# A graph network kernel: attention of 12 node tiles by slots instead of by edges

## The chip, the cores and the metric

The kernel runs on one core of a Trainium2 chip. The core has engines that run beside one another, each with its own queue of instructions: PE multiplies matrices, DVE and ACT work on rows of 128 partitions, POOL here issues the gathers and scatters that follow a list of indices, and SP issues plain DMAs. Sixteen DMA engines move the data. The time is the device's, in microseconds (us); the kernel before took 7391.83 us, the median of three runs (7389.55 to 7428.31).

## The reference, cut to what matters

A graph has 12500 nodes with 96 features and 200000 edges, sorted by destination. Four graph layers follow one another, each with a residual and a layer norm: L0 (mean over neighbours), L1 (two rounds of sums over neighbours), L2 (attention with 8 heads of 12 features, its edges' own features included), and L3 (a softmax over neighbours per feature). The layer that changes is L2:

```
Q_h = (x @ Wq + bq).reshape(N, H, D);  K_h = ...;  V_h = ...
E = (edge_attr @ We + be).reshape(-1, H, D)
score = K_h[src] * Q_h[dst] / sqrt(D) * E
score = exp(clip(score.sum(-1, keepdims=True), -5, 5))
wV = segment_sum(V_h[src] * score, dst);  Z = segment_sum(score, dst)
h_out = wV / (Z + 1e-6)
```

## The kernel before, in words

Nodes lie in 98 tiles of 128 (`NB`), edges in 1563 tiles of 128 (`NT`). Since edges are sorted, those of node tile `d` lie in edge tiles `16d-6` to `16d+21` (`reach`). There are two ways to bring a source's row to its edge.

*By edges.* POOL gathers, for each edge tile, 128 rows from DRAM by the list of sources, one instruction per tile. A one-hot matrix, made on DVE from the destinations, is multiplied with the rows on PE and sums them into the node tile.

*By slots.* In the first stage each edge of a node tile gets a place in a table of 25 groups (`SQ`) of 128 slots. A group serves four source tiles, 32 slots each (`granule`), so that a source's row can be picked by a one-hot matrix on PE from a table in SBUF; edges that find their 32 slots full go to 64 spare slots in the last group, whose rows POOL gathers (`gather_spares`). Two one-hot matrices per node tile, `ohT` (slot to source) and `ohd` (slot to destination), are made in the first stage, stored in DRAM (`ohT_d`, `ohd_d`) and read back by later passes.

The stages follow in time:

- The first stage (`passes`, `l0_nodes`, `edge_constants`, `edge_block`, `edge_steps`, `expand`, `first_sums`). It works out L0's products, the places of all edges, the one-hots, and L0's sums: the first 76 node tiles (`NS`) by slots, the other 22 by edges (`by_edges`, "others"). `edge_steps` goes through 64 edge tiles at a time; between them, one turn of `sums` per node tile. `spare` rows are gathered per node tile, `rows_e` in runs of up to 17 tiles.
- Two L1 passes (`whole_pass`), again 76 tiles by slots, 22 by edges. In the second, `l1_stage` also makes keys and values (`kv`, stored to `kv_d` as fp32) and queries (as two fp16 halves, `q_d`) of four node tiles at a time.
- `attention`, all tiles by edges, in 391 units of four edge tiles. `ask` gathers `kv` rows on POOL 8 units ahead (L1625, 12 buffers); `fetch` reads the edges' features `attr` and queries `qs` on SP 4 units ahead; `queries` makes the one-hot `ohq` on ACT from a row of destinations. `score` multiplies on PE the edges' features with We (`ep`, L1663) and one-hots with queries (`qp`, L1667), and on DVE their product with the keys (`s`, L1671 and L1672) and its sums per head (`sc`). `weigh` takes the exponential on ACT and weighs the values on DVE (`m`, L1686), which frees the unit's `kv`. `terms` splits `m` into two fp16 halves, `one_hots_of` makes `ohe` on DVE (L1703, four instructions per unit), and `scatter` sums on PE into the node tile's accumulator (`acc`, L1719). `done` and `stage` finish four node tiles at a time: they make the layer norm, and L3's table `ex`, which goes to DRAM (`ex_d`) and into a table in SBUF (`kept[2]`).
- L3 (`whole_pass`), 68 tiles by slots (`NS3`), 30 by edges.

In attention the order of PE, DVE, ACT and POOL is written out by hand (`manual_schedule`): in turn `u`, `ask(u + 8)`, `fetch(u + 4)`, `score(u)`, `weigh(u - 1)`, `terms(u - 2)`, `one_hots_of(u - 2)`, `queries(u + 3)`, one step of a `stage`, `scatter(u - 3)`. Elsewhere a planner sets the order by its own estimates, roughly that of the program. Each engine takes its queue in order, and a wait holds up what stands behind it. Waits for data and for free buffers are put in by the framework.

Of the kernel before, what the change touches and what calls it, by code (L numbers as in the profile page):

```python
# [23 lines left out]
P = 128  # L24
N = 12500
E = 200000
D = 96
# [503 lines left out]
NS3 = 68  # L531
TS = 16 * NS + 8
# [10 lines left out]
def gnn_fast(  # L543
# [67 lines left out]
    kv_d = dram.tile([NB * P, 2 * D], F32, name="kv_d")  # L611
    q_d = dram.tile([(NB + 1) * P, 2 * D], F16, name="q_d")
# [189 lines left out]
    def l0_nodes(work, psum, pieces):  # L802
# [3 lines left out]
        for g, n in node_batches():  # L806
            xg = work.tile([P, GB, D], F32, name="x0", bufs=2)
# [11 lines left out]
            own = work.tile([P, GB, D], F32, name="own0", bufs=2)  # L819
# [32 lines left out]
    def edge_constants(big):  # L852
# [7 lines left out]
        c.first = big.tile([P, NT], BF16, name="first")  # L860
        c.cont = big.tile([P, NT], BF16, name="cont")
        c.same = big.tile([P, NT], BF16, name="same")
# [16 lines left out]
        with tc.tile_pool(name="s_ord", bufs=1) as ordp, tc.tile_pool(name="s_ordp", bufs=2, space=PSUM) as psum:  # L879
# [24 lines left out]
            last = ordp.tile([P, NT], F32, name="last")  # L904
            for j0 in range(0, NT, 512):
                n = min(512, NT - j0)
                for k, to in enumerate((c.first, last)):
                    p = psum.tile([P, 512], F32, name="p")
                    nc.tensor.matmul(p[:, :n], ones_f[0:1, :], ends[:, k, j0 : j0 + n], start=True, stop=True)
                    nc.vector.tensor_copy(to[:, j0 : j0 + n], p[:, :n])  # L910
            nc.vector.memset(c.cont[:, 0:1], 0.0)
            nc.vector.tensor_tensor(c.cont[:, 1:], c.first[:, 1:], last[:, : NT - 1], op=ALU.is_equal)
# [30 lines left out]
    def edge_block(c, blk, psum, b0):  # L943
# [27 lines left out]
        if slots:  # L971
# [4 lines left out]
            t.rearrange("t (f i) -> t f i", i=4), rowf[:, 1].rearrange("t i f -> t f i"),  # L976
# [65 lines left out]
        b.j = blk.tile([P, BL], F32, name="j")  # L1042
# [7 lines left out]
    def edge_steps(c, work, psum, t0):  # L1050
# [80 lines left out]
        pg_all = pb.rearrange("p k (g i) -> p k g i", i=UE)  # L1131

# [41 lines left out]

    def expand(work, psum, placed, d):
# [3 lines left out]
        p = psum.tile([SQ, P], F32, name="tp")  # L1179
        nc.tensor.transpose(p, lo[:, :SQ], ident)  # L1180
        r = work.tile([SQ, P], BF16, name="lorow", bufs=2)
        nc.scalar.copy(r, p)
        nc.scalar.dma_start(rowd[d], r)
# [360 lines left out]
    def l1_stage(i):  # L1544
        def stage(work, psum, g, n, sums):
# [32 lines left out]
            nc.sync.dma_start(rows(kv_d, g, n), kv[:, :n, :])  # L1578
            nc.sync.dma_start(
# [6 lines left out]
    def attention():  # L1586
# [4 lines left out]
        CQ = 16  # L1591
        with ExitStack() as c2:
            cols, within = by_columns(c2.enter_context(tc.tile_pool(name="e_cols", bufs=1)), 0, NT, F32)
# [4 lines left out]
            accp = c2.enter_context(tc.tile_pool(name="e_acc", bufs=3, space=PSUM))  # L1598
# [5 lines left out]
            for i in range(6):  # L1604
                t = one.tile([D + 1, per * P], F32, name=f"attr{i}")
                nc.vector.memset(t[D : D + 1], 1.0)
                attr.append(t)
            units = [(t0, min(per, NT - t0)) for t0 in range(0, NT, per)]
            blocks, got, asked, early, acc, held = {}, {}, {}, {}, {}, {}

            def ask_block(b):
                if b * CQ < NT:
                    n = min(CQ, NT - b * CQ)
                    qb = work.tile([P, CQ * P], BF16, name="qb")
# [3 lines left out]
            def ask(u):  # L1618

                if u >= len(units):  # L1620
                    return
                t0, n = units[u]
                kv = uw.tile([P, per, 2 * D], F32, name="kv", bufs=EARLY + 4)
                for i in range(n):
                    nc.gpsimd.indirect_dma_start(  # L1625
                        out=kv[:, i, :], out_offset=None, in_=kv_d,
                        in_offset=bass.IndirectOffsetOnAxis(ap=cols[:, t0 + i : t0 + i + 1], axis=0),
# [3 lines left out]
            def fetch(u):  # L1631
# [4 lines left out]
                if t0 % CQ == 0:  # L1636
# [7 lines left out]
            def queries(u):  # L1644
# [4 lines left out]
                b = blocks[t0 // CQ][:, t0 % CQ * P : (t0 % CQ + n) * P]  # L1649
# [5 lines left out]

            def score(u):
                t0, n = units[u]
                a, qs = got.pop(u)
                ohq = asked.pop(u)
                kv = early.pop(u)  # L1660
                ep = psum.tile([P, per, D], F32, name="ep")
                for i in range(n):
                    nc.tensor.matmul(ep[:, i, :], a[:, i * P : (i + 1) * P], w_e, start=True, stop=True)  # L1663
                qp = psum.tile([P, per, D], F32, name="qp")
                for i in range(n):
# [4 lines left out]
                s = uw.tile([P, per, D], F32, name="s")  # L1670
                nc.vector.tensor_mul(s[:, :n, :], ep[:, :n, :], kv[:, :n, :D])  # L1671
                nc.vector.tensor_mul(s[:, :n, :], s[:, :n, :], qp[:, :n, :])  # L1672
                sc = uw.tile([P, per, HEADS], F32, name="sc", bufs=3)
                nc.vector.tensor_reduce(sc[:, :n, :], s[:, :n, :].rearrange("p e (h d) -> p e h d", d=HD), AX.X, ALU.add)  # L1674
                nc.vector.scalar_tensor_tensor(  # L1675
                    sc[:, :n, :], sc[:, :n, :], -5.0, five[:, :n, :], op0=ALU.max, op1=ALU.min
                )
                return n, kv, sc

            def weigh(n, kv, sc):  # L1680
# [3 lines left out]
                m = uw.tile([P, per, HEADS, H1], F32, name="m")  # L1684
                nc.scalar.mul(m[:, :n, :, HD], ex[:, :n, :], 2.0**8)
                nc.vector.tensor_mul(  # L1686
                    m[:, :n, :, :HD], kv[:, :n, D:].rearrange("p e (h d) -> p e h d", d=HD),
                    ex[:, :n, :, None].to_broadcast([P, n, HEADS, HD]),
                )
                return n, m.rearrange("p e h d -> p e (h d)")  # L1690

            def terms(n, m):
# [4 lines left out]
                return mh  # L1697

            def one_hots_of(u):
                t0, n = units[u]  # L1700
                o = uw.tile([P, per, 2 * P], BF16, name="ohe")
                for i in range(n):
                    nc.vector.tensor_scalar(o[:, i], wide, within[:, t0 + i : t0 + i + 1], None, op0=ALU.is_equal)  # L1703
                return o

            def scatter(u, m, ohe):
                t0, n = units[u]
                for i in range(n):
                    t = t0 + i
                    for k in range(2):  # L1710
                        d = nominal(t) + k
                        if not 0 <= d < NB:
# [13 lines left out]
            def done(d, a):  # L1726
# [258 lines left out]
```

## Time and profile before

The profiled execution took 7449.54 us; its span, from the first to the last instruction, is 7447.7 us. Times of the stages come from the windows view, whose columns give each engine's busy time.

| stage, us from the span's start | length | PE | DVE | ACT | POOL | clock granted to PE |
|---|---|---|---|---|---|---|
| first stage, 230 to 1575 | 1345 | 912.90 | 935.12 | 683.47 | 559.16 | 0.75 |
| L1, first pass, 1575 to 2560 | 985 | 634.62 | 372.07 | 283.31 | 399.24 | 0.75 |
| L1, second pass, 2560 to 3520 | 960 | 644.77 | 432.20 | 312.76 | 352.65 | 0.76 |
| attention, 3520 to 6075 | 2555 | 1376.31 | 1621.20 | 1007.41 | 1531.94 | 0.58 |
| L3, 6075 to 7448 | 1373 | 1004.79 | 636.33 | 454.79 | 496.37 | 0.80 |

A row of the windows view reads: start and end, length, then for each engine its busy time and its instructions (x), the granted share of PE's clock, the busy share of the DMA engines and their GB/s. A row of the view of waits reads: who waited, `<-`, for whom; total us, times, longest. A row of the timeline reads: start, duration, engine, line, operation, what it writes `<-` what it reads, how many, and in brackets how long the engine had been idle and who ended that. "Issue" means that the engine waited for nothing that the profile shows, "remote" that the releaser is unknown.

### The profile page before, as it was taken

What the parts mean: (1) busy time and instruction counts of PE and PEld (TensorE: products, weight loads), DVE (VectorE), ACT (ScalarE), POOL (GpSimd) and SP (SyncE); (2) the same over time, 40 slices, a digit from 0 to 9 for tenths busy, and PEclk for the clock granted to TensorE, in tenths of its full rate; (3) what the DMA queues carried; (4) which work ended last, traced back from release to release, by engine and by line L of the source; (5) the groups of instructions that cost most, each with busy time, mean ns of one, the idle gap of its engine ahead of it and who ended that gap; (6) DMA issues with size and microseconds to landing.
All of it is one profiled execution on the core that took longest, in us unless ns stands there. A gap on an engine that the chain in (4) does not pass through costs nothing.

```text
span 7447.7 us, 155952 instructions
## 1 busy us (share of the span) xinstructions
PE 4699.1 (63%) x63527; PEld 3396.2 (46%) x63527; DVE 4164.5 (56%) x9977; ACT 2805.0 (38%) x5549; POOL 3345.9 (45%) x3338
## 2 busy tenths in 40 slices
PE   5566776746666566666355555555555547777777
PEld 3454554534545444445344444444444434444444
DVE  7577777623434344445466666666666654444545
ACT  2454555523323233333244443444343433333333
POOL 0434444434343344332666565666666643333332
PEclk8677777767777777777555565655555658878888
DMA  4555555443434344444344444444444433333332
GB/s 104 151 163 167 163 167 165 149 116 103 112 99 112 96 110 112 118 119 130 109 129 130 125 131 127 130 132 127 128 130 130 131 90 90 88 88 90 90 89 62
DMA packets 656952, 894.05 MB, mean 120 GB/s; under 512 B 394162, under 2 KB 458885, under 8 KB 651357
## 3 DMA queue, kind: packets, MB, share of 16 engines
q1 hardware_dynamic: 498742, 615.02, 27.2%
q0 software_dynamic: 138784, 262.63, 14.3%
q8 instruction: 500, 8.19, 0.5%
q10 hardware_dynamic: 18695, 6.32, 0.4%
q14 instruction: 231, 1.89, 0.1%
HBM read 747.72 MB, written 135.87 MB: 119 GB/s over the span
## 4 chain that ended last, share of the span: by engine, by line
PE 29%; DVE 22%; another core or an unknown queue 15%; issue 13%; ACT 2%; POOL 1%; DMA 1%; DVEq 0%; ACTq 0%; SPq 0%; POOLq 0%
PE rows L1438 9%; PE acc L1449 7%; DVE ohe L1703 3%; PE acc L1369 3%; DVE s L1672 3%; DVE sc L1674 3%; DVE mh L1696 2%; DVE s L1671 2%; DVE msg L1441 2%; PE ep L1663 2%; PE acc L1719 2%; PE qp L1667 1%; POOL kv L1625 1%; DVE m L1686 1%
## 5 line engine op out<-in xcount | busy, mean ns | idle before, releaser
L1625 POOL DMA_INDIRECT kv<-kv_d,cols x1563 | 1531.4, 980 | 964.3 <-DVE m L1686 464.6
L1438 PE MATMUL rows<-tab,ohT 128*32 128x192 f16 (+1 forms) x21560 | 1114.2, 294 | 696.0 <-issue 610.9
L1441 ACT CAST msg<-rows 128x384 f16<-128x384 f32 (+1 forms) x1440 | 877.2, 641 | 1775.4 <-remote 1041.7
L1441 DVE CAST msg<-rows 128x768 f16<-128x768 f32 x720 | 686.7, 954 | 1478.7 <-remote 1008.1
L1383 POOL DMA_INDIRECT rows_e<-tab_d,cols x1065 | 1105.0, 1038 | 658.9 <-PE acc L1369 349.2
L1438 PEld LDWEIGHTS <-ohT 128*32 128x32 fp8e4 x21560 | 596.2, 101 | 1123.1 <-issue 1044.0
L1449 PE MATMUL acc<-msg,ohd 128*32 128x384 f16 (+1 forms) x10600 | 928.3, 324 | 247.8 <-issue 241.0
L1719 PE MATMUL acc<-mh,ohe 128*128 128x208 f16 x2727 | 516.3, 352 | 844.2 <-DVE ohe L1703 517.8
L1449 PEld LDWEIGHTS <-ohd 128*32 128x32 fp8e4 (+1 forms) x10600 | 554.0, 103 | 526.9 <-issue 434.7
L1719 PEld LDWEIGHTS <-ohe 128*128 128x128 bf16 x2727 | 293.3, 124 | 1011.0 <-DVE ohe L1703 575.5
L1663 PE MATMUL ep<-w_e,attr 97*128 97x96 f32 x3126 | 664.5, 382 | 35.3 <-issue 31.7
L1663 PEld LDWEIGHTS ep<-w_e,attr 97*128 97x128 f32 x3126 | 631.4, 297 | 37.6 <-issue 26.3
L1383 POOL DMA_INDIRECT rows_e<-ex_d,cols x483 | 464.2, 961 | 399.0 <-PE acc L1369 261.9
L1683 ACT ACTIVATE ex<-sc 128x32 f32<-128x32 f32 x391 | 89.7, 229 | 1440.5 <-DVE sc L1675 1166.9
L1303 ACT CAST msg<-rows 128x768 f16<-128x768 f32 x633 | 384.2, 644 | 459.8 <-PE rows L1299 224.6
L1671 DVE TENSOR_TENSOR s<-ep,kv 128x384 f32<-128x384 f32 x391 | 215.6, 551 | 604.7 <-remote 307.1
L1313 PE MATMUL acc<-msg,ohd 128*32 128x194 f16 x7600 | 389.3, 291 | 252.4 <-ACT msg L1303 177.9
L1667 PE MATMUL qp<-qs,ohq 128*128 128x96 f16 x3126 | 352.5, 260 | 292.9 <-issue 270.0
L1667 PEld LDWEIGHTS <-ohq 128*128 128x128 fp8e4 x3126 | 295.4, 136 | 339.4 <-issue 336.4
L1299 PE MATMUL rows<-tab,ohT 128*32 128x192 f16 x7448 | 393.9, 289 | 61.5 <-issue 59.6
L1242 POOL DMA_INDIRECT spare<-tab_d,spare_i x76 | 132.3, 1740 | 656.3 <-PE rows L1299 407.4
L1251 POOL DMA_INDIRECT spare<-tab_d,spare x76 | 72.0, 947 | 731.3 <-PE rows L1438 619.5
(697 smaller groups left out, 7604.9 us busy)
## 6 DMA issues: line engine op xcount, KB each, us to landing
ohT<-ohT_d SPq DMA_DIRECT2D x220, 400.0 KB
ohd<-ohd_d SPq DMA_DIRECT2D x220, 400.0 KB
attr<-cols_edge_attr_dram SPq DMA_DIRECT2D x390, 192.0 KB
bc<-rowd SPq DMA_DIRECT2D x76, 800.0 KB
qb<-qrow SPq DMA_DIRECT2D x97, 512.0 KB
sb<-srow SPq DMA_DIRECT2D x38, 1024.0 KB
ohd_d<-ohd SPq DMA_DIRECT2D x76, 400.0 KB
ohT_d<-ohT SPq DMA_DIRECT2D x76, 400.0 KB
```

The source lines that it names most:

```text
L1299: nc.tensor.matmul(ps[j * GR : (j + 1) * GR, i // R, i % R * W : (i % R + 1) * W], a, b, start=True, stop=True)
L1303: nc.scalar.copy(m[:, : n * R].rearrange("p (b r) t w -> p b (r t) w", r=R)[:, :, :, :D], ps[:, :n, : R * W].rearrange("p b (t w) -> p b t ...
L1313: nc.tensor.matmul(acc[d][j : j + GR, : W + 2], got[d][1][:, q, j : j + GR], m, start=(q == 0), stop=(q == SQ - 1))
L1383: nc.gpsimd.indirect_dma_start(out=m[:, i, :W], out_offset=None, in_=table, in_offset=bass.IndirectOffsetOnAxis(ap=rest_src[:, t : t + 1], ...
L1438: nc.tensor.matmul(ps[j * GR : (j + 1) * GR, i // R, i % R * W : (i % R + 1) * W], a, b, start=True, stop=True)
L1441: (nc.scalar.copy if engine else nc.vector.tensor_copy)(m, ps[:, :, : R * W])
L1449: nc.tensor.matmul(acc[d][j : j + wide, :W], got[d][1][:, q, j : j + wide], m, start=(q == 0), stop=(q == SQ - 1))
L1625: nc.gpsimd.indirect_dma_start(out=kv[:, i, :], out_offset=None, in_=kv_d, in_offset=bass.IndirectOffsetOnAxis(ap=cols[:, t0 + i : t0 + i ...
L1663: nc.tensor.matmul(ep[:, i, :], a[:, i * P : (i + 1) * P], w_e, start=True, stop=True)
L1667: nc.tensor.matmul(qp[:, i, :], ohq[:, i * P : (i + 1) * P], qs[:, t * D : (t + 1) * D], start=(t == 0), stop=(t == 1))
L1671: nc.vector.tensor_mul(s[:, :n, :], ep[:, :n, :], kv[:, :n, :D])
L1719: nc.tensor.matmul(acc[d].rearrange("p t w -> p (t w)"), ohe[:, i, k * P : (k + 1) * P], m[:, i].rearrange("p t w -> p (t w)"), start=(t = ...
```

## The change

Attention of the first 12 node tiles (`MS`) goes by slots. The edges' own terms, `edge_attr @ We + be`, of those tiles are worked out in the first stage (`edge_terms`): four edge tiles per step, one step per turn of `sums`, the result scattered by POOL to its slots in a new DRAM table `es_d`, which three DMAs on SP have filled with zeros before. The buffers that the terms pass through share a tag with two tiles of `l0_nodes` ("own0", four buffers). `edge_steps` works out each edge's slot number, `expand` also stores the destinations by slot (`rowq_d`), and `l1_stage` also stores `kv` as two fp16 halves (`kvh_d`). In attention a table of all `kvh` rows lies in SBUF; a slot unit takes four groups of slots, picks rows of it with `ohT`, multiplies with `es`, and sums with `ohd`. After 16 units by edges one slot unit follows about every fourth edge unit, until 24 before the end. The table's place in SBUF is L3's `kept[2]`, so batches of `ex` that are done before the last slot unit go to DRAM alone and are read back later (`bring`). Several rings in attention get shorter. Last, the host lays the edges of a tile out in one other order (edge 4f+i at position 32i+f), for all lists by columns. The diff, cut:

```diff
+MS = 12
-            xg = work.tile([P, GB, D], F32, name="x0", bufs=2)
+            xg = work.tile([P, GB, D], F32, name="own0", bufs=4)
...
+        if t0 < c.slot_i.shape[1]:
+            slot = small("at_")
+            nc.vector.tensor_add(slot, pb[:, 1, :n], c.nom[:, cs])
+            nc.vector.tensor_scalar(slot, slot, float(P), SD * ((t0 - c0) // 16) - 1.0, op0=ALU.mult, op1=ALU.add)
...
+    def edge_terms(c, work, psum):
+        last = reach(MS - 1)[1]
+        a = c.attr
+        nc.scalar.dma_start(a[:D, : UE * P], cols_attr[:, : UE * P])
+        for t0 in range(0, last + 1, UE):
+            yield
+            n = min(UE, last + 1 - t0)
+            p = psum.tile([P, UE, D], F32, name="tp")
+            for i in range(n):
+                nc.tensor.matmul(p[:, i, :], a[:, i * P : (i + 1) * P], w_e, start=True, stop=True)
+            e = work.tile([P, GB, D], F32, name="own0", bufs=4)
+            nc.scalar.copy(e[:, :n], p[:, :n])
+            if t0 + UE <= last:
+                m = min(UE, last + 1 - t0 - UE)
+                nc.scalar.dma_start(a[:D, : m * P], cols_attr[:, (t0 + UE) * P : (t0 + UE + m) * P])
+            for i in range(n):
+                st = nc.gpsimd.indirect_dma_start(
+                    out=es_d, out_offset=bass.IndirectOffsetOnAxis(ap=c.slot_i[:, t0 + i : t0 + i + 1], axis=0),
+                    in_=e[:, i, :], in_offset=None,
+                )
...
@@ l1_stage
             nc.sync.dma_start(rows(kv_d, g, n), kv[:, :n, :])
+            yield
+            kvh = work.tile([P, GB, 2, 2 * D], F16, name="kvh")
+            halves_of(kv[:, :n, :], kvh[:, :n])
+            nc.sync.dma_start(rows(kvh_d, g, n), kvh[:, :n].rearrange("p g t w -> p g (t w)"))
@@ attention
-            accp = c2.enter_context(tc.tile_pool(name="e_acc", bufs=3, space=PSUM))
+            accp = c2.enter_context(tc.tile_pool(name="e_acc", bufs=2, space=PSUM))
+            slotp = c2.enter_context(tc.tile_pool(name="e_slot", bufs=1, space=PSUM))
...
+            def fetch_slots(u):
+                g0 = units[u][0]
+                e = su.tile([P, UE, D], F32, name="es")
+                nc.sync.dma_start(e, es_d[g0 * P : (g0 + UE) * P].rearrange("(i p) w -> p i w", p=P))
...
-                kv = uw.tile([P, per, 2 * D], F32, name="kv", bufs=EARLY + 4)
+                kv = uw.tile([P, per, 2 * D], F32, name="kv", bufs=EARLY + 3)
...
+            def score_slots(u):
...
+                kvp = psum.tile([P, 2, 512], F32, name="eq")
+                kv = kvp[:, :, : 4 * D].rearrange("p b (r w) -> p b r w", r=2)
+                qp = slotp.tile([P, UE, D], F32, name="qp")
...
+                        for t in range(2):
+                            for j, (x, y) in enumerate(pairs):
+                                nc.tensor.matmul(
+                                    kvp[j * GR : (j + 1) * GR, i // 2, i % 2 * 2 * D : (i % 2 + 1) * 2 * D], x,
+                                    y[:, t * 2 * D : (t + 1) * 2 * D], start=(t == 0), stop=(t == 1),
+                                )
...
-                ep = psum.tile([P, per, D], F32, name="ep")
+                eq = psum.tile([P, 2, 512], F32, name="eq")
+                ep, qp = (eq[:, k, : per * D].rearrange("p (e w) -> p e w", e=per) for k in range(2))
...
+            def bring():
+                g, n = stored.pop(0)
+                nc.sync.dma_start(kept[2][0][g // CT][:, g % CT : g % CT + n], rows(ex_d, g, n))
...
             for u in range(4):
                 fetch(u)
+            kept["kv"] = load_table(tabp, kvh_d)
...
+                    if u == final:
+                        kept[2] = new_table(tabp, 4 * D, F16)
+                    if u > final + 2 and stored:
+                        bring()
...
@@ passes
+                    if k < MS // 4:
+                        to = es_d[4 * k * SD : 4 * (k + 1) * SD].rearrange("(p r c) w -> p r (c w)", p=P, c=2)
+                        nc.sync.dma_start(to, none[:, None, :].to_broadcast([P, 2 * SQ, 2 * D]))
+                    if k == MS // 4:
+                        next(terms_of)
...
-        kept[2] = new_table(pool, 4 * D, F16)
-        at_3 = without_slots(pool, NS3)
-        attention()
+        attention(pool)
+        cols3 = last3.enter_context(tc.tile_pool(name="h_cols", bufs=1))
+        at_3 = without_slots(cols3, NS3)
```

## The prediction

> **What bounds the kernel now.** I read the busy times by stage first, because the change takes work out of one stage and puts some into others.
>
> ```profile
> core 0: us, PE busy (x) PEld busy (x) DVE busy (x) ACT busy (x) POOL busy (x), PEclk, DMA share, GB/s
> 230.00:1575.00 1345.00, 912.90 (x18415) 677.28 (x18414) 935.12 (x2061) 683.47 (x1095) 559.16 (x432) 0.75 0.52 162
> ...
> 2560.00:3520.00 960.00, 644.77 (x10311) 443.40 (x10312) 432.20 (x931) 312.76 (x698) 352.65 (x369) 0.76 0.42 113
> 3520.00:6075.00 2555.00, 1376.31 (x8999) 1160.25 (x9000) 1621.20 (x4603) 1007.41 (x2128) 1531.94 (x1564) 0.58 0.45 127
> ```
>
> The rows are the first stage, the second L1 pass and attention. Attention is the longest, 2555 us, and no engine fills it: DVE is busy 1621 us, POOL 1532. It has 391 units of four edge tiles, so 6.53 us per unit, of which DVE works 4.15. The waits of that stage say who holds whom:
>
> ```profile
> POOL kv L1625 <- DVE m L1686: 464.6, 120, 11.0
> POOL kv L1625 <- issue: 407.8, 1320, 1.3
> ...
> DVE s L1671 <- remote: 307.1, 48, 15.0
> PE qp L1667 <- issue: 263.4, 336, 2.5
> ...
> DVE s L1671 <- PE qp L1667: 170.2, 25, 8.4
> DVE s L1672 <- remote: 168.7, 53, 5.7
> ```
>
> POOL's gathers of kv rows stop 120 times, until DVE frees a buffer; DVE stops for PE, or for something that the profile can't name. The order of time at one such place shows the two together:
>
> ```profile
> 3887.10 0.85 PE L1667 MATMUL qp<-qs,ohq 128*128 128x96 f16 x8
> ...
> 3889.90 0.95 POOL L1625 DMA_INDIRECT kv<-kv_d,cols  x1 [0.30 <-issue]
> ...
> 3892.91 0.56 DVE L1672 TENSOR_TENSOR s<-s,qp 128x384 f32<-128x384 f32 x1 [5.05 <-remote]
> ...
> 3895.01 1.05 POOL L1625 DMA_INDIRECT kv<-kv_d,cols  x1 [4.16 <-DVE m L1686]
> ```
>
> The qp products are done at 3888, yet DVE gets going at 3892.9, 2 us after POOL's last gather. So a run of gathers back to back (0.95 + 0.30 us each) holds PE, or the news of it, up. The L1 pass shows this best, in four stretches of about 21 us in which POOL gathers and rests in turn:
>
> ```profile
> 1999.00:2021.00 22.00, 9.73 (x105) 5.32 (x103) 6.45 (x16) 1.82 (x4) 15.69 (x16) 0.69 0.34 82
> 2021.00:2042.00 21.00, 19.52 (x388) 15.55 (x389) 13.86 (x28) 12.14 (x25) 1.88 (x2) 0.84 0.50 141
> 2042.00:2063.00 21.00, 10.34 (x100) 6.06 (x98) 3.58 (x11) 1.28 (x2) 15.26 (x16) 0.65 0.28 67
> 2063.00:2084.00 21.00, 17.76 (x365) 13.94 (x365) 13.09 (x24) 10.83 (x22) 1.02 (x2) 0.86 0.53 146
> ```
>
> With 16 gathers PE gets 100 matmuls through, with two 365 to 388. A long run costs about 15 us for 16 gathers, some 1 us per gather. Attention is therefore a cycle: about 12 gathers (15 us), a stop of about 5, three units done, 19.6 us.
>
> **The change part by part.** The profiled execution took 7449.54 us, its span 7447.7 (1.84 us lie around it); the median of the runs is 7391.83, 57.7 us less. I sum differences and put them on the median.
>
> *Attention, edge units.* The first 12 node tiles leave; edges start at tile 184, so 345 units remain of 391, with 1379 gathers of 1563, and 6 spare gathers come: 178 fewer on POOL. In their place come 12 x 25 / 4 = 75 slot units, one after about every fourth edge unit. DVE does for an edge unit 0.551 (s) + 0.554 (s) + 0.553 (sc) + 0.193 + 0.551 (m) + 0.583 (mh) + 4 x 0.301 (ohe) = 4.19 us; a slot unit has no ohe, 2.98 us. DVE: 75 x 2.98 - 46 x 4.19 = +31 us. ACT does the same for both. PE has 44 matmuls for a slot unit (32 rows, 8 qp, 4 acc) where an edge unit has 23 (8999 / 391), but the rows are cheap (40 of L1438 in 1.01 us at full clock, so 1.6 us for 32 at half), and 1.6 + 0.64 + 0.69 = 2.9 us fits beside DVE.
>
> What happens to the other 934 us of the stage (2555 - 1621) isn't shown. Three bounds. If POOL sets the pace, 178 gathers x 1.25 = -223 us. If each unit carries its idle time whatever its kind, 420 x 2.39 + 1652 = 2656, +101 us. If idle time goes with gathers, 934 x 1385 / 1563 = 828, and 828 + 1652 = 2480, -75 us. I take the last: the stretches above tie lost PE time to gathers, and those are the nearest row.
>
> *Attention, buffers.* A slot unit's kv rows stay in their PSUM pair until the product m, one unit later, where an edge unit frees its pair at the second product s. The ep matmuls of the unit after next wait for that, and behind them in PE's order its qp. DVE has 0.58 + 1.20 = 1.8 us (mh, ohe) to cover some 2.5 us of PE. Between 0 and 1.8 us x 75 = 135; I take 0.5 us, +37, since the cover is most of it. Fewer buffers for kv (11 for 12), attr, qb, s and m I cost at nothing: each is refilled four units ahead, some 26 us. SP issues about six DMAs of 0.35 us for a slot unit and two for an edge unit, and now waits for PE to free attr most of the time; if that cover went, SP's queue would hold attr and es up together, and the edge units with them.
>
> *First stage.* Terms of 198 edge tiles in 50 steps, one per node tile. PE: 8 fp32 records in 1.46 to 1.90 us in attention (ep), say 1.3 at this stage's clock, 65 us. ACT: 50 x 0.52 (a copy of 128x384) + 50 issues of attr at about 0.4 = 46 us; SP's issues took 0.32 to 0.48. DVE: 10 small operations in four rounds at some 0.22, 9 us. POOL: 198 scatters x 1.25 = 248 us on top of 559 of 1345. No engine is full (PE 68%, DVE 70%), so I put half of PE's and ACT's 111 us on the path, +55, between 0 and 111. The scatters wait for ACT's copy, and behind them stand POOL's gathers of spares and rows_e; they also lengthen the runs of gathers. At 1 us per gather that is up to 198 us; runs of four cost nothing to see, so I take +20. The fills of the store with zeros are 3 x 4.9 MB on SP's queue ahead of the loads of sb, cb and bc. At this stage's 162 GB/s they last 91 us, beside 48% idle DMA; +10, between 0 and 60, as the ramp up to 330 us has nothing else to do while bc is late. Sum +85.
>
> A rule that speaks against this part: the Trainium skill's "DMA: Bandwidth & Descriptors" (Specifications) has writes below 512 bytes done as read-modify-write, and each scattered row is 384 bytes. No run here shows such a scatter. If that doubled each scatter's time on the DMA engines it would be an estimate of 198 us more of transfers beside others, which moves the sum only where POOL must wait for them.
>
> *Second L1 pass.* Per batch of four tiles one more ACT copy and one DVE subtraction of 128x768, a DMA of 393 KB on SP, and one step more in the tail. ACT's cast of that size takes 0.64 and DVE's 0.95: 25 x 1.6 = 40 us if nothing hides it, 0 if all. Between two casts each engine has 0.7 to 0.9 us idle waiting for PE, so +12.
>
> *Both ends of attention.* The table of 9.6 MB is loaded at the start by 7 DMAs on SP and 6 on ACT's queue, ahead of attr from the fifth unit on. At the 215 GB/s of 3520 to 3540 that is 45 us. It lies beside the opening run of 32 gathers, in which PE rests until 3591 already: +8, between 0 and 45. At the end some 23 batches of four tiles of ex are read back, one per unit, beside 24 units of 6 us, and the last one or two stand on the path (+4). The columns for L3 are loaded after attention, where they cost about 9 us (3522 to 3531); POOL waits for them, its gathers come that much later, PE has slots to go on with: +4. Sum +16.
>
> The new order of edges within tiles, shorter constants and the second transpose for 12 tiles: below 5 us each way, 0.
>
> Total -75 + 37 + 85 + 12 + 16 = **+75 us**: 7391.8 + 75 = 7467, so 7465.
>
> **The rivals.**
> 1. *POOL paces attention.* Then the slot units lie in POOL's shadow: -223, no wait at PSUM, the rest at its low end (first stage +30, others +15): -178, 7214. For it: 1563 x 1.25 = 1954 us of gathers in 2555, the tightest engine. Against it: POOL itself waits 465 us for DVE. It decides once runs of gathers get shorter than about 9 us, because slot units break them up; then PE is never held.
> 2. *POOL's queue becomes the bound of the first stage.* A turn lasts 17.5 us; POOL has 7.4 of it, with the scatters 12.4, in longer runs. A spare gather behind four scatters comes 5 us late, and the rows of that tile with it. At 50 x 4 us this stage is +200 rather than +85: 7582. Against it: POOL idles 786 us there.
> 3. *Slot units carry an edge unit's idle time.* They have twice PE's instructions, and if a run of gathers lets only so many through, they drain it sooner: +101 instead of -75, 7643.
>
> **How the numbers follow.** A measurement here can't tell less than 0.5% (37 us) from no change. Forecast 0.43 (0.31 slower, 0.12 within: its parts reach from +0 to +170); rival 1 0.27 (0.25 faster, 0.02 within); rival 2 0.17, slower; rival 3 0.13 (0.10 slower, 0.03 within, where the first stage stays at its low end). Slower 0.58, same 0.17, faster 0.25. The range, 7260 to 7640, reaches from most of rival 1 to rival 3; the forecast's own is 7390 to 7560.
>
> **What would show it.** Attention about 2520 us with some 103 to 110 stops of POOL for DVE's m; DVE about 1650 us there; the first stage about 85 us longer, POOL about 800 us busy in it; the second pass 10 to 15 longer. The forecast is wrong if attention falls by over 150 us, with few waits of s for "remote" (rival 1); if the waits of spare or rows in the first stage grow past 100 us (rival 2); or if PE's qp and rows wait for "issue" more than 264 us in all in attention (rival 3).

## The result and the profile after

The changed kernel takes 7682.76 us (median of four runs, 7674.27 to 7697.55), the kernel before 7400.54 (four runs): 1.0378 of it, 95% interval 1.0343 to 1.0413. It is slower by 282 us. The forecast, 7465, had the sign, but less than a third of the loss, and its range ended at 7640.

The windows view of the kernel after, by stage (columns as before; the first row is the ramp, up to the first product of slots, the last row attention):

```profile
core 0: us, PE busy (x) PEld busy (x) DVE busy (x) ACT busy (x) POOL busy (x), PEclk, DMA share, GB/s
0.00:343.00 343.00, 153.94 (x928) 116.98 (x928) 258.14 (x584) 67.08 (x292) 6.66 (x38) 0.73 0.51 148
343.00:1849.00 1506.00, 984.75 (x18501) 733.24 (x18500) 854.40 (x1941) 703.25 (x1141) 787.32 (x629) 0.73 0.48 151
...
2815.00:3780.00 965.00, 663.81 (x10317) 450.26 (x10317) 450.45 (x954) 329.65 (x723) 361.40 (x373) 0.76 0.42 122
3780.00:6298.00 2518.00, 1477.92 (x11211) 1120.85 (x11210) 1657.93 (x4570) 1006.22 (x2266) 1375.53 (x1387) 0.61 0.48 135
```

The stages stand next to the forecast like this: the first stage ends at 1849 instead of 1577, 272 us later (forecast 85). It grew at both its ends: the ramp is 343 us instead of 230, and from there to the end it is 1506 instead of 1347. The two L1 passes take 1930 us instead of 1942. Attention, from its first product to its last, takes 2518 instead of 2546; L3 is as long as it was. Together that is 235 us, the difference of the two profiled executions; that of the kernel before, 7449.54, lay 58 us above its median, so these lengths are not the median's. All of the loss is in the first stage, and attention won next to nothing. The waits of attention after (L1786 makes a slot unit's rows and L1791 its `qp`, L1818 an edge unit's `ep` and L1821 its `qp`):

```profile
POOL kv L1727 <- DVE m L1838: 660.9, 155, 9.6
POOL kv L1727 <- issue: 361.6, 1185, 0.5
DVE s L1796 <- remote: 299.5, 38, 10.1
...
DVE s L1825 <- remote: 228.1, 28, 34.8
...
PE eq L1818 <- issue: 161.9, 135, 12.2
...
PE eq L1786 <- issue: 94.5, 141, 1.9
...
PE eq L1821 <- issue: 73.6, 90, 2.6
...
PE qp L1791 <- issue: 36.3, 56, 1.8
```

It is still the cycle of the profile before: POOL stops for `m`, now 155 times and 661 us, where it was 120 times and 465, and DVE stops for a releaser that isn't named. Three waits of the first stage before, after its ramp:

```profile
POOL spare L1242 <- PE rows L1299: 407.4, 45, 17.0
...
ACT msg L1303 <- remote: 176.6, 44, 12.4
...
PE rows L1299 <- issue: 61.8, 115, 2.5
```

And those of the first stage after:

```profile
ACT msg L1349 <- remote: 297.1, 62, 31.9
...
POOL spare L1288 <- PE rows L1345: 287.1, 42, 14.7
...
POOL es_d L1210 <- ACT own L1205: 93.5, 16, 14.4
PE rows L1345 <- issue: 90.5, 156, 1.8
...
POOL es_d L1210 <- issue: 52.1, 171, 0.3
```

POOL still waits 287 us for PE's rows (407 before): its queue isn't full. PE's wait for issue at the rows (62 before, 91 now) and ACT's wait for an unnamed releaser (177 before, 297 now) have grown. One scatter lasts about as long on POOL as a gather of attention before (median 946 ns):

```profile
L1210 POOL DMA_INDIRECT es_d<-own,slot_i x198: 964/987/4029, 604.2 to 1607.4; - x198
```

### The profile page after: what moved, and what is told of

The parts are those of the page before. It is cut to its first block, busy times and chain, and to the rows that moved or that the text cites. A ratio compares the mean times of both kernels' runs of the same rounds, so it can differ in the third digit from the quotient of the medians.

```text
span 7682.7 us, 161844 instructions
## 1 busy us (share of the span) xinstructions
PE 4911.4 (64%) x66165; PEld 3440.9 (45%) x66165; DVE 4240.0 (55%) x10030; ACT 2849.2 (37%) x5769; POOL 3424.5 (45%) x3358
## 4 chain that ended last, share of the span: by engine, by line
PE 32%; DVE 18%; issue 18%; another core or an unknown queue 16%; POOL 8%; ACT 4%; DMA 3%; SPq 0%; ACTq 0%; DVEq 0%; POOLq 0%
PE rows L1484 9%; POOL kv L1727 8%; PE acc L1495 7%; PE acc L1415 3%; PE acc L1359 2%; DVE msg L1487 2%; PE rows L1345 2%; ACT msg L1349 1%; DVE ohe L1859 1%; DVE sc L1802 1%; DVE mh L1850 1%; DVE s L1826 1%; PE tp L1567 1%; DVE s L1825 1%
## 5 line engine op out<-in xcount | busy, mean ns | idle before, releaser
L1727 POOL DMA_INDIRECT kv<-kv_d,cols x1379 | 1367.1, 991 | 1047.5 <-DVE m L1838 660.9
L1887 PE MATMUL acc<-mh,ohe 128*128 128x208 f16 x2397 | 473.5, 348 | 484.7 <-DVE ohe L1859 213.9
L1818 PE MATMUL eq<-w_e,attr 97*128 97x96 f32 x2758 | 596.9, 380 | 207.8 <-issue 161.9
L1818 PEld LDWEIGHTS eq<-w_e,attr 97*128 97x128 f32 x2758 | 551.3, 290 | 266.1 <-issue 238.8
L1887 PEld LDWEIGHTS <-ohe 128*128 128x128 bf16 x2397 | 265.9, 127 | 619.5 <-issue 235.8
L1359 PEld LDWEIGHTS <-ohd 128*32 128x32 fp8e4 x7600 | 223.2, 111 | 356.8 <-issue 341.3
L1288 POOL DMA_INDIRECT spare<-tab_d,spare_i x76 | 116.2, 1530 | 594.1 <-DMA ohT_d<-ohT 293.9
L1415 PE MATMUL acc<-rows_e,ones_e 128*128 128x192 f16 (+2 forms) x2644 | 347.8, 284 | 44.7 <-issue 23.6
L1825 DVE TENSOR_TENSOR s<-eq,kv 128x384 f32<-128x384 f32 x345 | 190.5, 552 | 322.0 <-remote 228.1
```

Of the source, the lines that this page charges most:

```text
L1359: nc.tensor.matmul(acc[d][j : j + GR, : W + 2], got[d][1][:, q, j : j + GR], m, start=(q == 0), stop=(q == SQ - 1))
L1415: nc.tensor.matmul(acc[:, : W + count], ones[:, :, i], rows_of[u][:, t % UE + i, : W + count], start=(t + i == first), stop=(t + i == last),)
L1727: nc.gpsimd.indirect_dma_start(out=kv[:, i, :], out_offset=None, in_=kv_d, in_offset=bass.IndirectOffsetOnAxis(ap=cols[:, t0 + i - first_t ...
L1887: nc.tensor.matmul(acc[d].rearrange("p t w -> p (t w)"), ohe[:, i, k * P : (k + 1) * P], m[:, i].rearrange("p t w -> p (t w)"), start=(t = ...
```

## The experiments

One fact has to come first, as no number can be read without it. The runs fell on chips of two kinds. On one (call it A: the first comparison, and one chip for the runs a0, b0, e6, e7, f1 and f2) the kernel before takes 7389 to 7450 us. On the other (B, four chips) it takes 5294 to 5322. Each ratio is against the kernel before on the same chip. That it is the chip, and not something that held while these runs went on, is the simplest reading and was not tested. What differs between A and B is told at the end of this section.

**Four edits, on B.** The first took out the scatters, the second the terms altogether:

```diff
-            for i in range(n):
-                st = nc.gpsimd.indirect_dma_start(
-                    out=es_d, out_offset=bass.IndirectOffsetOnAxis(ap=c.slot_i[:, t0 + i : t0 + i + 1], axis=0),
...
-                terms_of = edge_terms(c, work, psum)
+                terms_of = iter(())
```

The third set the three fills to the start of the program, and the fourth gave `l0_nodes` its two rings back:

```diff
+            for k in range(MS // 4):
+                to = es_d[4 * k * SD : 4 * (k + 1) * SD].rearrange("(p r c) w -> p r (c w)", p=P, c=2)
+                nc.sync.dma_start(to, none[:, None, :].to_broadcast([P, 2 * SQ, 2 * D]))
             none_h = none.bitcast(F16)
...
-            xg = work.tile([P, GB, D], F32, name="own0", bufs=4)
+            xg = work.tile([P, GB, D], F32, name="x0", bufs=2)
...
-            own = work.tile([P, GB, D], F32, name="own0", bufs=4)
+            own = work.tile([P, GB, D], F32, name="own0", bufs=2)
...
-            e = work.tile([P, GB, D], F32, name="own0", bufs=4)
+            e = work.tile([P, GB, D], F32, name="own0", bufs=2)
```

> The changed kernel without the 198 scatters of edge terms into the store: the products, ACT's copies and attr's loads stay, the store holds only its zeros, so attention sees no edge terms for the first 12 node tiles. The ramp (until the first rows of slots, 343 us) is untouched by this. Theory S, the scatters on POOL's queue cost the steady part of the first stage: it falls by 110 to 160 of the 159 us that it grew, the kernel to about 7550. Theory W, it is the work of PE and ACT for the terms that costs: at most 30 us go, 7655 or more.

> The changed kernel without the edge terms at all (no products, copies, loads of attr or scatters; the zero fills and the slot numbers stay). Theory S: within 20 us of the kernel that lacks only the scatters. Theory W: 100 us or more below it. By the prediction's own terms (half of 111 us of PE and ACT, 20 for longer runs) it would be 75 us below the changed kernel, 7610, and the one without scatters 20 below, 7660.

> The changed kernel with the three zero fills issued at the start, right after the zeros are set, ahead of the edge blocks: they then move their 14.7 MB while the DMA engines idle (40 to 75 us) instead of at 104 to 150 us. Theory F, the fills hold up the ramp: first rows of slots at 280 us or earlier, the kernel 50 to 80 us faster. Theory R, the shared ring of l0_nodes' loads and stores holds it up: first rows within 20 us of 343, the kernel within 20 us of the changed one.

> The changed kernel with x and own of l0_nodes in two rings of two buffers again, as before, instead of one ring of four (edge terms take own's two). Theory R, in one ring the load of the next x can only be asked for once own of this batch has its buffer, so loads are no longer ahead: first rows of slots back at 240 to 270 us, the kernel 70 to 110 us faster. Theory F: first rows later than 310 us, less than 30 us faster. If the two buffers hold up the edge terms the steady part grows; ACT's waits at the terms' copy would show it.

Measured, as ratios: no scatters 0.9843 (0.9826 to 0.9860), no terms 0.9701 (0.9680 to 0.9722), early fills 1.0017 (1.0007 to 1.0027), two rings 0.9910 (0.9894 to 0.9927). The first rows of slots come at 346, 346, 360 and 241 us. It is the one ring that holds up the ramp (theory R): with two rings, and the fills where they were, it is 241 us, 15 more than in the kernel before on B. The time gained 57 us where 70 to 110 were expected. The run with early fills says little by itself. They stood at the start of the program, but SP waited 65 us there for DVE and issued them at 72 to 100 us instead of 71 to 130; the ramp became 14 us longer. The absolute times in these expectations were written for A; in their place, scatters cost 92 us here and the rest of the terms 80, so neither theory S nor theory W holds alone. Both are measured from the kernel with early fills, which stands in for the changed kernel; beside that itself, on another chip of B (runs g1 and g2 below), the scatters are 78.

**The changed kernel and the one ring, on A.** Two of the next four are the changed kernel and the kernel before as they are. The third sets the one ring into the kernel before, with x and `own` both as "own0" with four buffers. The fourth gives the changed kernel two rings and lets the terms use both:

```diff
-            e = work.tile([P, GB, D], F32, name="own0", bufs=4)
+            e = work.tile([P, GB, D], F32, name=("x0", "own0")[t0 // UE % 2], bufs=2)
```

> The changed kernel as it is, on the chip of these runs. The kernel with early fills took 1.002 of before there, and its first rows of slots came at 360 us, so the fills had not held up the ramp. If the change costs here what it cost in the first comparison, the ratio is 1.038. If a part of that cost belongs to the chip, on which a run of gathers took PE to a standstill (before takes 5306 us here and 7392 there), it is 1.000 to 1.010, about 5320 us if before takes 5306.

> The kernel before, for its profile on this chip. If runs of gathers hold PE up here too, stretches with 16 gathers have some 100 matmuls against 388 without, as in the first profile; if not, PE keeps 15 matmuls or more per us through them, the waits named remote and issue are far below the 1041 us (ACT's msg) and 611 us (PE's rows) of the first profile, and attention, no longer paced by that, is bound by DVE.

> The kernel before with one edit of the change alone: x and own of l0_nodes in one ring of four buffers. Theory R: loads no longer run ahead, first rows of slots some 80 to 110 us later than in the kernel before, and the time 40 to 100 us longer (part of the ramp's edge blocks is done meanwhile and is saved later). If the ring does not matter: within 10 us.

> The changed kernel with two rings of two buffers for x and own, and the edge terms taking one of each in turn, so that they have four buffers at the same memory. With own's two alone ACT waited 110 us for scatters to free one. If that wait is on the path, 30 to 60 us faster than two rings alone (0.991 of before): 0.980 to 0.985. If it only moved to POOL's queue: within 10 us of it.

Measured: the changed kernel 1.0379 (1.0355 to 1.0402), the first result again; the kernel before 7408.95, a single run; the one ring alone 1.0002 (0.9993 to 1.0012), where 40 to 100 us were expected; both rings 1.0257 (1.0226 to 1.0288). The last of these expectations, 0.980 to 0.985, was for B, and its two parts can't be told apart on A. On B both rings (run h2, 0.9907) then came out as two rings alone did (0.9910): there, ACT's wait had only moved.

How the ring works shows in SP's timeline of the changed kernel (L813 loads x, L842 stores `own`; start, duration, line, how many):

```profile
6.97 0.41 SPq L813 DMA_DIRECT2D own<-in_x_dram  x1
...
87.57 1.19 SPq L842 DMA_DIRECT2D own_d<-own  x1
...
103.64 0.43 SPq L813 DMA_DIRECT2D own<-in_x_dram  x1
...
118.79 1.06 SPq L842 DMA_DIRECT2D own_d<-own  x1
...
121.75 0.90 SPq L813 DMA_DIRECT2D own<-in_x_dram  x1
```

and in that of the kernel before on the same chip (L809 loads x, L838 stores `own`):

```profile
6.73 70.70 SPq L809 DMA_DIRECT2D x<-in_x_dram  x3
...
79.22 2.88 SPq L809 DMA_DIRECT2D x<-in_x_dram  x2
...
95.66 0.43 SPq L838 DMA_DIRECT2D own_d<-own  x1
```

Before, five loads are out ahead of the first store. With one ring, buffers are handed out in the order x, `own`, x, `own`, so the next x gets its buffer only after this batch's `own` has got its own; one load is out, and the second is issued after the first store. The ring has as many buffers as the two had, and yet nothing is loaded ahead.

What that costs is a second question. In the kernel before on A, the one ring made the ramp 316 us instead of 230, and the first stage ended at 1576 instead of 1570. The ramp wasn't empty: DVE did 252 us of work in it instead of 167, and the rest of the stage became shorter by 80. The rows of that kernel:

```profile
0.00:316.00 316.00, 157.37 (x930) 120.75 (x930) 252.27 (x545) 67.12 (x294) 6.54 (x38) 0.72 0.41 114
316.00:1576.00 1260.00, 854.78 (x18104) 643.71 (x18106) 850.81 (x1947) 676.30 (x1089) 566.29 (x432) 0.77 0.54 165
```

and of the changed kernel with both rings:

```profile
0.00:242.00 242.00, 111.34 (x476) 84.55 (x480) 140.32 (x373) 62.79 (x278) 10.65 (x41) 0.72 0.51 139
242.00:1763.00 1521.00, 991.91 (x18967) 738.40 (x18963) 971.83 (x2151) 708.13 (x1155) 817.28 (x626) 0.75 0.52 161
```

Here the rest of the stage takes 1521 us, with one ring 1506: 117 us more of DVE's work in it, and only 15 us more time. So with the terms the ring's 104 us of ramp stay lost, all but 15; the first stage ends at 1851 with it (run a0) and at 1763 without, 88 us.

**Scatters and terms, on A.** The same two cuts as on B, from the kernel with both rings.

> The changed kernel with both rings of two for x and own (terms in turn), and without the 198 scatters, so that attention sees no edge terms for the first 12 node tiles. To be set against the same with scatters (1.0257 of before where a run of gathers holds PE up; first stage 1763 us). Theory S, there 198 scatters lengthen the runs in which PE stands still by about 1 us each, the bound that the prediction gave and put at 20: the first stage falls by 130 to 200, the ratio to about 1.003. Theory Q, the scatters cost only their place in POOL's queue, as where PE runs on through gathers (92 us of 5318 there): 60 to 90 us, ratio 1.015.

> The same without the edge terms at all (no products, copies, loads of attr, scatters). What is left of the change in the first stage is fills, slot numbers and shorter constants. Theory W, PE's and ACT's work for the terms lies on the path: 50 to 111 us below the one that lacks only the scatters (80 us where PE runs on through gathers). Half of 111 us, +55, was the prediction's term. If all of the loss is in the terms, the first stage is within 20 us of the kernel before (1570 us where that takes 7410) and the ratio 0.985 to 1.000.

Without scatters 1.0063 (1.0040 to 1.0086), the first stage 1626 us; without terms 1.0012 (0.9999 to 1.0025), where 0.985 to 1.000 was expected, 1577. Theory S had 130 to 200 us for the scatters, theory Q 60 to 90: it is 137. The work of PE and ACT is 49. And without the terms and the ring nothing is left: 1577 against 1570. Two waits of the first stage differ with it, with scatters:

```profile
ACT msg L1349 <- remote: 234.8, 44, 20.8
...
PE rows L1345 <- issue: 91.9, 150, 2.5
```

and without:

```profile
ACT msg L1342 <- remote: 110.1, 29, 15.2
...
PE rows L1338 <- issue: 59.7, 89, 2.5
```

They are 125 and 32 us longer with the scatters. From the traces, the time in which POOL issues two or more indirect DMAs back to back (less than 0.6 us between them), after the ramp, is 928 us of this stage with the scatters and 574 without. Runs of 20 and more are 12 with the scatters and 1 without. PE starts 10.7 and 10.1 matmuls per us in such time, and 15.3 and 16.1 outside it. In the same kernel on B (run h2) it starts 15.7 in it and 14.0 outside, so it is not what the kernel does in a run that makes PE slow there. On A the 354 us more of such time, at 30 to 37% of PE's rate lost, are an estimated 107 to 131 us, most of the 137. That PE's rate is what the stage's length follows is argued, not tested by itself.

**On B, the whole account.** The remaining runs have no new edits but combine those above: the one ring without scatters, both rings, both rings without terms, the one ring in the kernel before, and the two kernels themselves.

> The changed kernel without the 198 scatters, with its one ring for x and own (so attention sees no edge terms for the first 12 node tiles); to be set against the two rings without scatters (first stage 1626 us, 1.006 of before where before takes 7410). In the kernel before the one ring lengthened the ramp by 86 us and the steady part gave 79 back, as 95 us of DVE's work was done in the ramp; with all of the terms nothing came back (88 us). Theory P, what takes the gain away is that POOL's scatters, not DVE, pace the steady part: without them most comes back, first stage 1630 to 1660, ratio 1.007 to 1.012. Theory T, any step of terms per turn does it: first stage 1700 or later, ratio 1.016 or more.

> The changed kernel once more beside the kernel before, for the chip on which before takes 5306 us: there the kernel with early fills took 1.002 of it and stood for this one. On that chip: 1.000 to 1.010. On one where before takes some 7400: 1.038 again, and it adds to the interval.

> The kernel before, for its profile on that chip. Where before takes 5306 us: PE passes 15 matmuls or more per us through runs of gathers, and attention with what follows it is at least 150 us longer than the 2679 us of the changed kernel there, for the changed kernel has to win 172 us for the terms and 57 for the ring back to come out at 1.002.

> One ring, no scatters, as before (attention sees no edge terms for the first 12 node tiles). Where before takes some 7400 us it answers what stayed open. Theory P (POOL's scatters, not DVE, pace the steady part, so that DVE's work done in the ramp saves nothing): without them most of the ring's 88 us comes back, first stage 1630 to 1660 us, ratio 1.007 to 1.012. Theory T (any step of terms per turn does it): 1700 or later, 1.016 or more. Where before takes 5306: 0.985 once more.

> Two rings, the terms using both in turn (1.0257 where before takes 7420). Where before takes 5306: the one ring cost 57 us at 5318 against two with the terms in own's two buffers, where ACT waited 110 us for one; with four buffers 0 to 30 us less than that, ratio 0.985 to 0.992.

> Two rings, no edge terms (so attention sees none for the first 12 node tiles); 1.0012 where before takes 7410. Where before takes 5306: if the terms and the ring are the whole loss of the first stage (199 us), its first stage is within 20 us of before's 1301 us, and the gain of attention (225 us) stays: ratio 0.957 to 0.965.

> One ring, no scatters (attention sees no edge terms for the first 12 node tiles), for a chip on which before takes some 7400 us. Theory P (POOL's scatters pace the steady part there, so that work done ahead in the ramp saves nothing): first stage 1630 to 1660 us, ratio 1.007 to 1.012. Theory T (any step of terms per turn does it): 1700 or later, 1.016 or more. Where before takes 5306: 0.984 to 0.985 again.

> The kernel before with the one ring alone, for a chip on which before takes 5306 us. There the one ring cost 16 us of the first stage without the terms (1339 to 1355) and 36 with them (1464 to 1500): 10 to 25 us, ratio 1.002 to 1.005. Where before takes 7420: 1.000 again.

The changed kernel takes 0.9988 (0.9978 to 0.9998) here, both rings 0.9907 (0.9885 to 0.9930), both rings without terms 0.9666 (0.9649 to 0.9683), the kernel before with one ring 1.0047 (1.0031 to 1.0063), one ring without scatters 0.9848, 0.9837 and 0.9831. The kernel before took 5314.53 in its profiled run. Without terms and ring the first stage ends 38 us after that of the kernel before, where within 20 was expected. The ends of the first stage side by side:

| kernel | A, us | B, us |
|---|---|---|
| before | 1570 | 1301 |
| before, one ring | 1576 | 1319 |
| changed, two rings, no terms | 1577 | 1339 |
| changed, one ring, no terms | not run | 1355 |
| changed, two rings, no scatters | 1626 | not run |
| changed, one ring, no scatters | not run | 1427 to 1440 |
| changed, two rings | 1763 | 1464 |
| changed | 1851 | 1500 |

On B the first stage loses 199 us: 38 for what is left when terms and ring are gone, 16 for the ring, 72 to 85 for the products and copies, 60 to 73 for the scatters. On A it is 7, 49, 137 and 88, 281 in all (the order of the cuts differs: on A the ring is taken last, on B first; last, it is 36 there). Run i2 answered that the ring isn't free on B even without terms, 18 us. What stays open is whether on A the ring's 88 belong to the scatters or to any step of the terms: the run that tells, one ring without scatters, fell on B all four times. All that the traces add is that on A POOL's scatters wait 100 us for ACT's copies with one ring (run a0) and 19 with both (run e7).

On B the scatters cost in another way. Of the 1155 us after the ramp POOL issues back to back for 1042 (on A, 887 of 1506), and PE waits for the spare rows, which POOL gathers in the same queue. With the scatters (run g2), and without (run g1, the same chip):

```profile
PE rows L1345 <- DMA spare<-tab_d,spare_i: 76.5, 16, 13.2
```

```profile
PE rows L1338 <- DMA spare<-tab_d,spare_i: 11.9, 1, 11.9
```

These 65 us more are about what the scatters cost there. It is the way of the second rival, POOL's queue as the bound. On A the waits of the first stage hold no such wait of PE, neither with one ring nor with both.

And attention? On B it goes from 2048 us to 1823, by 225 us. The rows of attention before and after, on B:

```profile
2413.00:4461.00 2048.00, 1377.25 (x8976) 1223.55 (x8976) 1641.57 (x4580) 1003.13 (x2123) 1550.31 (x1564) 0.57 0.56 157
```

```profile
2620.00:4443.00 1823.00, 1279.35 (x11213) 1009.59 (x11212) 1655.46 (x4571) 1005.18 (x2265) 1381.42 (x1387) 0.70 0.68 186
```

DVE has the same work in both, but in the second it is busy 91% of the time instead of 80%. The waits of the kernel before in it, on B:

```profile
POOL kv L1625 <- issue: 384.8, 1263, 0.3
DVE s L1671 <- DMA kv<-kv_d,cols: 255.3, 240, 5.2
...
POOL kv L1625 <- DVE m L1686: 18.3, 60, 0.3
```

POOL never stops for `m` for more than 0.3 us; it issues gathers without a break, 1550 us of them and 385 between them, and DVE waits for the rows. There POOL paces attention, as the first rival had it, and the 225 us are the rival's price of 178 gathers, 223.

**What differs between A and B** shows best in three stretches of 21 us of an L1 pass of the kernel before, on B:

```profile
1700.00:1721.00 21.00, 20.18 (x412) 16.88 (x408) 18.51 (x43) 12.60 (x29) 16.12 (x17) 1.00 0.71 192
1721.00:1742.00 21.00, 20.46 (x483) 17.23 (x480) 13.95 (x26) 11.60 (x24) 16.12 (x17) 1.00 0.76 210
1742.00:1763.00 21.00, 18.74 (x408) 15.64 (x400) 14.19 (x31) 11.24 (x22) 16.12 (x17) 1.00 0.69 181
```

POOL has 17 gathers in each and PE passes 408 to 483 matmuls. In the profile before, on A, 16 gathers left it some 100. Over both L1 passes, PE starts 5.0 matmuls per us on A (run b0) while two or more gathers go back to back, 925 us of the time, and 16.0 in the rest. On B (run g3) POOL gathers so for 1005 us, and PE starts 19.6 per us in them. Whole L1 passes take 1936 us on A and 1112 on B. The program is the same, and so is the work of the other engines (the kernel before, A and B: DVE 4164 and 4176 us busy, ACT 2805 and 2792).

## Why the prediction was wrong, step by step

*That runs of gathers hold PE up.* Right for A, where all four stretches were read, and where both L1 passes show it as a whole (5.0 matmuls per us against 16.0); it is the basis of most other steps. It was told as the behaviour of a run of gathers, and it is that of a run of gathers on A.

*Attention, both ends included: -75 + 37 + 16 = -22.* Measured on A -28 in the first pair and -5 in the second, with 3 to 4 us more in L3. In three profiles on A attention of the kernel before lasts 2546, 2521 and 2524 us (the last with one ring), that of the changed kernel 2519 and 2516, and 2537 with both rings. So a gain of 22 us can't be told from none, and that the first pair fits the sum may be luck. Of the +16 for the ends, the 8 for the load of the table didn't come: the 16th product `m` starts 167 to 171 us into attention, in the kernel before 172 and 173. The 4 at the end and the 4 in L3 fit (3 to 5 us over the last 24 units, 3 to 4 in L3). DVE's 1650 came out at 1658, the length of 2520 at 2518. The stops for `m` didn't: 103 to 110 were forecast, and there are 155, so a slot unit doesn't leave them out as the forecast had it. What the -75 and the +37 are worth apart was not tested.

*First stage, products and copies: +55.* Measured +49 on A (72 to 85 on B).

*First stage, zero fills: +10, between 0 and 60.* 7 on A for the fills, slot numbers and shorter constants together, 38 on B. With two rings the ramp, fills included, is 13 us longer than in the kernel before on A (run f2, 243 against 230), so that they do not set it.

*First stage, scatters: +20, between 0 and 198.* This is the first of the two failed steps: 137. The prediction had the price, 1 us of PE's time per gather in a run, and the bound that follows from it, 198. Then it set that aside because "runs of four cost nothing to see". The scatters do not stand alone as runs of four: they join the runs that were there. In the kernel with both rings 190 of the 198 stand in runs of five or more and 8 in runs of four, and the time in runs grew by 354 us, of which the scatters themselves are busy 284.

*First stage, buffers: nothing.* The second failed step, 88 us on A when it is taken out last, and it wasn't in the sum at all. The diff shows the shared tag; the prediction says nothing of it and did not ask in which order the buffers are handed out. No bound of the prediction covers it. With 137 in place of 20 and 88 in place of nothing the sum would be 280, where 282 were measured; that it fits so closely is luck, as other terms were off by up to 24 us. The range was passed by 43 us.

*Second L1 pass: +12.* Measured for both passes -7 to -12 on A and +7 on B; on A the added copy, subtraction and DMA are hidden.

*Read-modify-write.* The prediction set the rule of the Trainium skill, "DMA: Bandwidth & Descriptors" (Specifications), against the scatter's 384-byte rows. The trace doesn't show the doubling that was weighed. With the scatters (run e7) the first stage has 3168 more records of eight such rows on the gathers' and scatters' queue than without (run f1), and 421 us more of the DMA engines' time: 0.13 us for each, where the others took 0.23. Over 16 engines that is 26 us each, so even doubled they would have weighed far less than the 198 of the prediction's estimate. This is the transfer's time alone, not what the memory does behind it.

*The rivals.* Rival 1 was wrong on A and right on B: -225 us of attention, where it gave -223, because there PE is never held. Its condition was named ("then PE is never held"), and its cause was not: not shorter runs but another chip. Rival 2 came nearest to the stage's loss on A (+200 against 272), but not in its way: POOL idles 719 us there (786 before), 287 of them for PE's rows, and PE doesn't wait for spares. Its way is what B shows, at 65 us. Rival 3 would have made attention longer by over 100 us, and on A it got 5 to 28 shorter. Its sign alone doesn't settle it: PE's `qp` and rows wait 204 us for issue (95, 74 and 36), under the 264 that it named, but `ep` went from 32 to 162, and all of these together from 302 to 366.

## What to carry to other kernels

When an edit merges two rings of buffers, write out the order in which buffers are handed out: as many buffers as before can still mean that nothing is loaded ahead, and then ask what the engines do in the delay, for a ramp that was 86 us longer cost 6 us in one kernel here, and one that was 104 longer cost 88 in another. Price an added indirect DMA by the run that it joins, not by the run that it makes. And don't put a term near nothing when the profile gives it a bound of 198, until a row shows the work hidden: it measured 137, where the products, put at half of their bound of 111, measured 49.

Of the versions with all of the work, those with two rings are the fastest on B, 0.9907 and 0.9910 of the kernel before; on A none is faster than the kernel before.

## What was not expected of the hardware

One program takes 7407 us on one chip and 5313 on another (profiled executions of the kernel before). PE's granted clock is 0.71 on A and 0.78 on B, which doesn't explain 16 gathers with 100 matmuls against 17 with 408 to 483. The packets that carry instructions take the same on both, 0.95 us (median of 744 and 745), and a gather of attention on POOL 0.98 to 0.99. What holds PE on A in a run of gathers is not in any record, and stays open. For the change this decides: it takes 38 per thousand more on A and, with an interval of 0.2 to 2.2, 1.2 per thousand less on B.
